# Four blocks of a two-turn macaron layer: transposes moved from TensorE to VectorE squares, with fewer steps in between

## The chip, the cores and the metric

The kernel runs on one core of a Trainium2 chip. The metric is the device time of one execution in microseconds (us). A core has engines that run side by side and meet at semaphores: TensorE (PE, matrix products; its weight loads are listed as PEld), VectorE (DVE), ScalarE (ACT), GpSimd (POOL) and SyncE (SP, which here only issues transfers). Transfers (DMAs) are issued by SP and by GpSimd. Matmul results land in PSUM, which holds eight banks of 128x512 fp32 numbers here; everything else lies in SBUF or in the chip's DRAM.

## What is computed

The input x has 4 sequences of 1024 positions with 256 features. The reference is three residual parts, each after a layer norm:

```
x = x + 0.5 * ffn(layernorm(x))
x = x + attn(layernorm(x))          # long convolution over positions, gelu, @ W.T + b
x = x + 0.5 * ffn(layernorm(x))     # the same weights as the first

def ffn(x):                         # weights are ternary, with one scale per output
    h = silu(lin(x, w1)) * lin(x, w2)     # 256 -> 1024
    h = gelu(lin(h, h1))                  # 1024 -> 1024
    h = gelu(lin(h, h2))                  # 1024 -> 1024
    return lin(h, w3)                     # 1024 -> 256
```

## The kernel before

**Two turns of eight blocks.** The 4096 positions are cut into 8 blocks of 512. The first turn ("f", names with _f) runs the first ffn over the eight blocks and leaves x1 in DRAM; the second turn ("g", names with _g) runs the last ffn on x2 and writes the output. The convolution part ("mixing", `mix`, one run per sequence of two blocks) turns x1 into x2; it is cut into small pieces that are put between the steps of the ffn of later blocks, by a planner (`tick`) that gives each step an allowance of 2500 units of work and counts every VectorE operation as 130 plus its columns. Checks that no weight is changed by the rounding to fp32r (`given`, `weight_checks`) fill what is left; their verdict passes through one small matmul, `p_bad`.

**The ffn of a block.** Activations are kept with features on the partitions and positions along the columns, as two fp32r parts: a rounded part, and the low part that is left over. `linear` (L355) makes an output tile of 128x512 from 2 x k matmuls, one per part and per 128 inputs. Layer 1 makes 8 pairs of tiles `pa`, `pb` from the block's normalized input `xt`; layers 2 and 3 make 8 tiles each, `p`, of 16 matmuls; the last makes `po`, 32 matmuls. After each tile of layers 2 and 3, ScalarE applies gelu (L388) and rounds (L390), and VectorE makes the low part (L293, `low_part`).

**Steps.** After each of these 16 tiles the ffn calls `ahead`, which moves the preparation of the next block on by one step: 16 steps, and a last one in front of `po`. `prepare` is a generator; each `yield` in it ends a step.

**Preparing a block.** It loads the next block's x, takes statistics, applies the root on ScalarE, scales (`norm`), and has to turn positions-by-features into features-by-positions, `xt`. There are two ways:

- *On TensorE* (`transposed`, L295). `load_rows` brings the block in one DMA, with 128 positions on the partitions. In the last step, eight 128x128 transposes into two PSUM banks `pt` (L302), then VectorE copies the rounded part out of PSUM (L312) and makes the low part (L293).
- *In squares* (`squares`, L317, and `parted`, L340). `load_x` brings the block in four DMAs of 128 KB, ordered so that VectorE's transpose of 32x32 squares puts each square where four stores to a DRAM buffer `moved` (L328, issued by GpSimd) can place it; after both halves, two loads `xf` (L336, GpSimd) bring features-by-positions back. In the last step VectorE rounds `xf` into `xt` (L345) and makes the low part (L293).

Before the change all blocks of the first turn but block 0, and the odd blocks of the second turn, are made in squares; the even blocks of the second turn (0, 2, 4, 6) are made on TensorE. Block 0 of the first turn is made on TensorE too, at the start of the kernel. The odd and the even blocks start at different steps, because mixing leaves x2 two blocks at a time: an odd block loads at once, an even one waits nine steps first. What one step issues:

| step | odd block, squares | even block, TensorE |
|---|---|---|
| 1 | load (4 DMAs) | |
| 4 | statistics, root | |
| 6 | scaling | |
| 8, 9 | square transposes, stores to `moved` | |
| 10 | | load (1 DMA) |
| 11 | loads of `xf` | |
| 13 | | statistics, root |
| 15 | | scaling |
| last | round, low part | 8 transposes, copies, low part |

The program is written in this order, but a scheduler puts each engine's instructions into a fixed order of its own, so that an instruction can stand earlier or later in its engine's queue than its step.

**Buffers.** `xb` (the loaded block) has 3 buffers, shared with the mixing's inputs; `half` tiles (among them `sq` and `xf`) 19, `ring` tiles (`xt` and the activations) 15, PSUM 8.

**Two programs in one.** If the weight checks find something, a second copy of the kernel with full fp32 arithmetic runs; with these inputs it doesn't.

Of the kernel before, what the change touches and what calls it, by code (L numbers as in the profile page):

```python
# [11 lines left out]
F32 = mybir.dt.float32  # L12
# [5 lines left out]
P = 128  # L18
B, L, D = 4, 1024, 256
HID = 1024  # L20
J = L // P
DC = D // P
KH = HID // P
TB = 512
JT = TB // P
# [72 lines left out]
def macaron_layers(  # L98
# [23 lines left out]
    nc = tc.nc  # L122
    split = bad is not None
# [3 lines left out]
    work = ctx.enter_context(tc.tile_pool(name="work", bufs=2))  # L127
# [21 lines left out]
    def bank(name):  # L149
        return psum.tile([P, 512], F32, tag="ps", name=name)  # L150

    def half(name, *shape, dtype=F32):

        return work.tile([P, *(shape or (512,))], dtype, tag="half", name=name, bufs=19)

    def ring(name, *shape, dtype=F32):

        return work.tile([P, *shape], dtype, tag="ring", name=name, bufs=15)
# [5 lines left out]
    ident = keep.tile([P, P], F32, name="ident")  # L164
# [14 lines left out]
    x2 = dram.tile([B, L, D], F32, name="x2")  # L179
# [17 lines left out]
    def block_of(t, blk):  # L197
        b, g = divmod(blk, J // JT)
        return t[b, g * TB : (g + 1) * TB, :]

    def tokens(t, blk, i=0, n=JT):

        return block_of(t, blk).rearrange("(i p) d -> p i d", p=P)[:, i : i + n, :]
# [3 lines left out]
        src = block_of(t, blk).rearrange("(n s) (q r) -> q s n r", s=SQ, r=SQ)  # L207
        return src[k * (P // SQ) + c]

    def load_rows(t, blk, name):  # L210

        xb = work.tile([P, JT, D], F32, tag="xb", name=name, bufs=3)
        nc.sync.dma_start(xb, tokens(t, blk))
        return xb

    def load_x(t, blk, name, queue=nc.sync):


        xb = work.tile([P, JT, D], F32, tag="xb", name=name, bufs=3)
        src = block_of(t, blk).rearrange("(i n s) d -> i s n d", i=JT, s=SQ)  # L220
        for i in range(JT):
            queue.dma_start(xb[i * SQ : (i + 1) * SQ], src[i])
        return xb
# [9 lines left out]
    x_first = work.tile([P, JT, D], F32, tag="xb", name="x_f0", bufs=3)  # L233
# [27 lines left out]
    def norm(t, name, parts_of=1):  # L261

        stats = small.tile([P, JT, 6], F32, tag="stats", name=f"stats_{name}", bufs=3)
        mv = small.tile([P, JT, 2], F32, tag="mv", name=f"mv_{name}", bufs=3)
        rstd = small.tile([P, JT], F32, tag="rstd", name=f"rstd_{name}", bufs=3)
        step = JT // parts_of
        for at in range(0, JT, step):
            here = range(at, at + step)
            for i in here:
                bn_stats(stats[:, i, :], t[:, i, :])  # L270
            for i in here:
                bn_aggr(mv[:, i, :], stats[:, i, :])
            nc.scalar.activation(
                rstd[:, at : at + step], mv[:, at : at + step, 1], AF.Sqrt, bias=eps
            )
        yield
        for at in range(0, JT, step):
            nc.vector.reciprocal(rstd[:, at : at + step], rstd[:, at : at + step])
            for i in range(at, at + step):
                ts(  # L280
                    t[:, i, :],
                    t[:, i, :],
                    mv[:, i, 0:1],
                    rstd[:, i : i + 1],
                    ALU.subtract,
                    ALU.mult,
                )
        yield


    def low_part(t, src):

        return nc.vector.tensor_tensor(t[:, 1, :], src, t[:, 0, :].bitcast(F32), ALU.subtract)  # L293

    def transposed(xn, name, first=False):  # L295

        pts = [bank(f"pt_{name}_{k}") for k in range(DC)]
        order = [(k, i) for k in range(DC) for i in range(JT)]  # L300
        for k, i in sorted(order, key=lambda o: o[1]) if first else order:
            nc.tensor.transpose(  # L302
                pts[k][:, i * P : (i + 1) * P], xn[:, i, k * P : (k + 1) * P], ident
            )
        xt = [ring(f"xt_{name}_{k}", parts, TB, dtype=wide) for k in range(DC)]
        last = None
        if first:
            last = nc.vector.tensor_copy(xt[0][:, 0, :], pts[0])  # L308
            nc.scalar.copy(xt[1][:, 0, :], pts[1])
        for k in range(DC):  # L310
            if not first:
                nc.vector.tensor_copy(xt[k][:, 0, :], pts[k])  # L312
            if split:
                last = low_part(xt[k], pts[k])
        return (xt, last) if first else xt

    def squares(xn, name):  # L317

        out = []
        for k in range(DC):
            sq = half(f"sq_{name}_{k}", P // SQ, JT, SQ)
            squares_of(
                sq, xn[:, :, k * P : (k + 1) * P].rearrange("p j (c r) -> p c j r", r=SQ)
            )
            for a in range(JT):
                stores.dma_start(  # L328
                    moved[k].rearrange("(c r) a q -> a r c q", r=SQ)[a],
                    sq[a * SQ : (a + 1) * SQ].rearrange("r c j s -> r c (j s)"),  # L330
                )
            yield
        yield
        for k in range(DC):
            t = half(f"xf_{name}_{k}")
            stores.dma_start(t, moved[k].rearrange("d a q -> d (a q)"))  # L336
            out.append(t)
        yield out

    def parted(xf, name):  # L340

        xt = []
        for k, src in enumerate(xf):
            t = ring(f"xt_{name}_{k}", parts, TB, dtype=wide)
            nc.vector.tensor_copy(t[:, 0, :], src)  # L345
            if split:
                low_part(t, src)
            xt.append(t)
        return xt
# [617 lines left out]
    def prepare(turn, blk, upcoming):  # L967

        name = f"{turn}{blk}"

        by_squares = turn == "f" or blk % 2 == 1
        if turn == "f":

            queue = weights_from if blk < 4 else nc.sync
            xb = x_second if blk == 1 else load_x(x, blk, f"x_{name}", queue)
        else:
            if not by_squares:
                for _ in range(9):
                    yield
            while ("m", blk // 2) not in done:  # L980
                next(aside, None)
            xb = (load_x if by_squares else load_rows)(x2, blk, f"x_{name}")
        yield
        yield
        yield
        for _ in norm(xb, name):
            yield
            yield
        if by_squares:
            for xf in squares(xb, name):  # L990
                yield
        while ("last layer", blk, turn) not in done:
            yield
        upcoming.extend(parted(xf, name) if by_squares else transposed(xb, name))

    def all_aside():

# [36 lines left out]
        nc.tensor.matmul(warm[:, 0:P], ident, ident, start=(i == 0), stop=(i == N_WARM - 1))  # L1034
    for _ in norm(x_first, "f0", parts_of=2):
        pass
    xt, last_split = transposed(x_first, "f0", first=True)
    allowed = work_done
    for n, (turn, blk) in enumerate(blocks):
        following = []  # L1040
        steps = [prepare(*b, following) for b in blocks[n + 1 : n + 2]]

        def ahead(last=False):
            for step in steps:
                if last:
                    done.append(("last layer", *blocks[n + 1][::-1]))
                next(step, None)

        src, dst = (x, x1) if turn == "f" else (x2, out)
        with tc.issue_after(last_split.ins) if n == 0 else nullcontext():  # L1050
            ffn(xt, src, dst, blk, f"{turn}{blk}", tick, ahead, n + 1 == len(blocks))
        done.append((turn, blk))
        xt = following
# [5 lines left out]
def macaron_kernel(tc: tile.TileContext, *args):  # L1059
    nc = tc.nc  # L1060
    with tc.tile_pool(name="flag", bufs=1) as flags:
        bad = flags.tile([1, 1], I32, name="bad")
        macaron_layers(tc, bad, *args)
        n_bad = nc.values_load(bad, min_val=0, max_val=1 << 24)
        with tc.If(n_bad > 0):
            macaron_layers(tc, None, *args)
# [65 lines left out]
```

## Time and profile before

| | |
|---|---|
| time, median of 3 runs | 1409.93 us (1409.23 to 1410.16) |
| the profiled execution | 1409.72 us |
| its span, first to last instruction | 1407.9 us |
| granted clock of TensorE | 0.999 of full speed |
| VectorE's 8 casts of `xt` from PSUM (L312) | 687 ns each |
| VectorE's 8 casts of `xt` from `xf`, second turn (L345) | 423 ns each |
| square transposes of 128x512, second turn | 705 ns each |
| GpSimd's issues to `moved`, second turn | 32, 551 ns each |
| matmuls of layers 2 and 3, second turn | 2048, 390 to 391 ns each |

The span is what the profile covers; the execution's own time is 1.82 us longer. A mean length isn't what an instruction holds an engine for: 390 ns is the length of a matmul from start to end, but they overlap, and 1024 of them are busy 236.5 us together, 0.23 us each. So for TensorE starts are compared with starts. "Idle before" and "waited" count the time in which an engine stood still ahead of an instruction, and name what released it.

In the second turn a block takes 79 to 94 us, which depends on how much mixing lies between its steps. VectorE is busy 48 to 63 us of each of the first four blocks, and about 26 us of block 6, which has no mixing.

### The profile page before, as it was taken

What the parts mean: (1) busy time and instruction counts of PE and PEld (TensorE: products, weight loads), DVE (VectorE), ACT (ScalarE), POOL (GpSimd) and SP (SyncE); (2) the same over time, 40 slices, a digit from 0 to 9 for tenths busy, and PEclk for the clock granted to TensorE, in tenths of its full rate; (3) what the DMA queues carried; (4) which work ended last, traced back from release to release, by engine and by line L of the source; (5) the groups of instructions that cost most, each with busy time, mean ns of one, the idle gap of its engine ahead of it and who ended that gap; (6) DMA issues with size and microseconds to landing.
All of it is one profiled execution on the core that took longest, in us unless ns stands there. A gap on an engine that the chain in (4) does not pass through costs nothing.

```text
span 1407.9 us, 17823 instructions
## 1 busy us (share of the span) xinstructions
PE 1397.6 (99%) x6524; PEld 1165.4 (83%) x6524; DVE 836.2 (59%) x1606; ACT 708.4 (50%) x1070; POOL 244.2 (17%) x358
## 2 busy tenths in 40 slices
PE   9999999999999999999999999999999999999997
PEld 7888888888888888888888888888888888888886
DVE  6896567755547784477673568744586744542412
ACT  5986479644546454344352553533545343553532
POOL 4221012211312120320113200214002122021200
PEclk9999999999999999999999999999999999999999
DMA  9401101122231322422113304034031223111000
GB/s 357 113 19 29 33 16 46 30 57 68 72 90 36 115 66 70 135 60 83 34 46 116 105 31 112 23 120 112 23 93 35 60 68 108 54 32 40 16 15 19
DMA packets 109282, 97.06 MB, mean 69 GB/s; under 512 B 71472, under 2 KB 81712, under 8 KB 109184
## 3 DMA queue, kind: packets, MB, share of 16 engines
q1 hardware_dynamic: 93056, 55.37, 14.3%
q0 software_dynamic: 15856, 40.19, 9.9%
q8 instruction: 53, 0.87, 0.3%
q14 instruction: 45, 0.37, 0.1%
q10 hardware_dynamic: 272, 0.26, 0.1%
HBM read 74.81 MB, written 20.97 MB: 68 GB/s over the span
## 4 chain that ended last, share of the span: by engine, by line
PE 99%; DVE 0%; POOL 0%; issue 0%; POOLq 0%
PE p_f L355 33%; PE p_g L355 33%; PE pa_f L355 4%; PE po_f L355 4%; PE pb_f L355 4%; PE pb_g L355 4%; PE pa_g L355 4%; PE po_g L355 4%; PE pi L916 2%; PE pw L941 2%; PE pf_m L738 2%; PE pk L665 1%; PE po_g L434 1%; PE pf_k L738 0%; PE warm L1034 0%; PE pt_g L302 0%
## 5 line engine op out<-in xcount | busy, mean ns | idle before, releaser
L355 PE MATMUL p_f<-h_f,h_sb 128*128 128x512 f32 x1024 | 237.2, 391 | 0.0
L355 PE MATMUL p_g<-ha_g,h_sb 128*128 128x512 f32 x1024 | 236.5, 391 | 0.0
L355 PE MATMUL p_g<-h_g,h_sb 128*128 128x512 f32 x1024 | 235.6, 390 | 0.0
L355 PE MATMUL p_f<-ha_f,h_sb 128*128 128x512 f32 x1024 | 235.3, 390 | 0.0
L293 DVE TENSOR_TENSOR h_g<-g_g,h_g 128x512 fp32r<-128x512 f32 x128 | 88.5, 692 | 246.5 <-ACT h_g L390 246.3
L388 ACT ACTIVATE g_g<-p_g,sc_sb 128x512 f32<-128x512 f32 x128 | 88.3, 690 | 275.9 <-PE p_g L355 268.9
L355 PEld LDWEIGHTS p_g<-ha_g,h_sb 128*128 128x128 f32 x1024 | 192.0, 188 | 40.5 <-DVE ha_g L293 0.9
L355 PEld LDWEIGHTS p_f<-h_f,h_sb 128*128 128x128 f32 x1024 | 191.8, 188 | 40.1 <-DVE h_f L293 0.3
L355 PEld LDWEIGHTS p_g<-h_g,h_sb 128*128 128x128 f32 x1024 | 192.0, 188 | 39.8
L355 PEld LDWEIGHTS p_f<-ha_f,h_sb 128*128 128x128 f32 x1024 | 191.9, 188 | 39.8
L388 ACT ACTIVATE g_f<-p_f,sc_sb 128x512 f32<-128x512 f32 x128 | 87.7, 689 | 188.9 <-PE p_f L355 188.5
L293 DVE TENSOR_TENSOR h_f<-g_f,h_f 128x512 fp32r<-128x512 f32 x128 | 87.8, 690 | 145.8 <-ACT h_f L390 145.4
L390 ACT CAST h_g<-g_g 128x512 fp32r<-128x512 f32 x128 | 79.4, 620 | 4.0
L390 ACT CAST h_f<-g_f 128x512 fp32r<-128x512 f32 x128 | 78.3, 618 | 3.0
L388 ACT ACT_TABLE_LOAD x51 | 65.4, 1283 | 25.0 <-PE p_f L355 14.3
L355 PE MATMUL pa_f<-xt_f,w_sb 128*128 128x512 f32 x256 | 69.1, 390 | 0.6 <-DVE xt_f L308 0.6
L417 POOL TENSOR_TENSOR y_g<-xr_g,y_g 128x512 f32<-128x512 f32 x14 | 18.1, 1294 | 293.1 <-DVE y_g L416 293.0
L355 PE MATMUL pb_f<-xt_f,w_sb 128*128 128x512 f32 x256 | 68.8, 389 | 0.0
L355 PE MATMUL pa_g<-xt_g,w_sb 128*128 128x512 f32 x256 | 68.4, 389 | 0.0
L355 PE MATMUL pb_g<-xt_g,w_sb 128*128 128x512 f32 x256 | 68.4, 389 | 0.0
L374 DVE SCALAR_TENSOR_TENSOR g_g<-pb_g,sc_sb,g_g 128x512 f32<-128x512 f32 x64 | 47.9, 749 | 27.8 <-PE pb_g L355 16.6
L328 POOL DMA_DIRECT2D moved<-sq_f x56 | 30.8, 556 | 182.9 <-DVE sq_f L140 182.9
(238 smaller groups left out, 1847.0 us busy)
## 6 DMA issues: line engine op xcount, KB each, us to landing
h_sb<-in_h_dram POOLq DMA_DIRECT2D x8, 1024.0 KB, 14.3
given<-in_h_dram SPq DMA_DIRECT2D x32, 256.0 KB, 3.8
kr<-k_hat SPq DMA_DIRECT2D x20, 256.0 KB, 2.6
ki<-k_hat SPq DMA_DIRECT2D x20, 256.0 KB, 2.9
xr_f<-in_x_dram SPq DMA_DIRECT2D x64, 64.0 KB, 2.4
x<-y_f POOLq DMA_DIRECT2D x64, 64.0 KB, 2.1
xm<-x SPq DMA_DIRECT2D x8, 512.0 KB, 3.7
m_m<-in_cosm_dram SPq DMA_DIRECT2D x16, 256.0 KB, 4.4
```

Source lines behind the costliest of these rows:

```text
L293: return nc.vector.tensor_tensor(t[:, 1, :], src, t[:, 0, :].bitcast(F32), ALU.subtract)
L328: stores.dma_start(moved[k].rearrange("(c r) a q -> a r c q", r=SQ)[a], sq[a * SQ : (a + 1) * SQ].rearrange("r c j s -> r c (j s)"),)
L355: nc.tensor.matmul(ps, w[:, k, m * P : (m + 1) * P], acts[k][:, part, :], start=(k == 0 and part == 0), stop=(k == n - 1 and part == parts ...
L374: nc.vector.scalar_tensor_tensor(g if split else t[:, 0, :], pb, sc_sb[:, 1, m : m + 1], g, ALU.mult, ALU.mult)
L388: nc.scalar.activation(g, ps, AF.Gelu, scale=sc_sb[:, layer, m : m + 1])
L390: nc.scalar.copy(t[:, 0, :], g)
L417: nc.gpsimd.tensor_tensor(y, rest[k], y, ALU.add)
L434: nc.tensor.matmul(ps[:, e * D : (e + 1) * D], ha[k][:, part, (i + e) * P : (i + e + 1) * P], w3_sb[:, k, :], start=(k == 0 and part == 0) ...
L665: nc.tensor.matmul(pk[0:NA, at + i, :, :].rearrange("p h b -> p (h b)"), a[:, i].rearrange("p a b -> p (a b)"), qd[d1 // per_tile][:, at + ...
L738: nc.tensor.matmul(ps[e][:, part, :], m[:, e, part, :], rows_of(q + JQ * e), start=True, stop=True)
L916: nc.tensor.matmul(banks[dc][e][:, q * P : (q + 1) * P], vs[q + JQ * e][:, part, dc * P : (dc + 1) * P], m[:, e, part, :], start=(part == ...
L941: nc.tensor.matmul(ps[:, e * D : (e + 1) * D], yts[dc][j // JQ][:, (j % JQ + e) * P : (j % JQ + e + 1) * P], wt_sb[:, dc, :], start=(dc == 0),
```

## The change

The even blocks of the second turn go the way of the odd ones: `load_x`, `norm`, `squares`, `parted`. To fit in, their preparation begins after seven steps and not nine, and some of the empty steps between its parts are left out: two steps and not three after the load, and one and not two after each half of `norm`. So an even block now loads at step 8, takes statistics at 10, scales at 11, transposes squares at 12 and 13, loads `xf` at 15, and rounds in the last step. The odd blocks' steps stay. `load_rows` goes, and `transposed` keeps only the form that block 0 of the first turn uses. The core of the diff:

```diff
-    def load_rows(t, blk, name):
-
-        xb = work.tile([P, JT, D], F32, tag="xb", name=name, bufs=3)
-        nc.sync.dma_start(xb, tokens(t, blk))
-        return xb
...
-        by_squares = turn == "f" or blk % 2 == 1
+        late = turn == "g" and blk % 2 == 0
         if turn == "f":
 
             queue = weights_from if blk < 4 else nc.sync
             xb = x_second if blk == 1 else load_x(x, blk, f"x_{name}", queue)
         else:
-            if not by_squares:
-                for _ in range(9):
+            if late:
+                for _ in range(7):
                     yield
             while ("m", blk // 2) not in done:
                 next(aside, None)
-            xb = (load_x if by_squares else load_rows)(x2, blk, f"x_{name}")
-        yield
-        yield
-        yield
+            xb = load_x(x2, blk, f"x_{name}")
+        yield
+        yield
+        if not late:
+            yield
         for _ in norm(xb, name):
             yield
+            if not late:
+                yield
+        for xf in squares(xb, name):
             yield
-        if by_squares:
-            for xf in squares(xb, name):
-                yield
         while ("last layer", blk, turn) not in done:
             yield
-        upcoming.extend(parted(xf, name) if by_squares else transposed(xb, name))
+        upcoming.extend(parted(xf, name))
```

The functions it calls, `load_x`, `norm`, `squares` and `parted`, are unchanged.

More of the change, by code (lines that the diff above doesn't have):

```diff
@@ L293, in low_part, with transposed @@
         return nc.vector.tensor_tensor(t[:, 1, :], src, t[:, 0, :].bitcast(F32), ALU.subtract)
-    def transposed(xn, name, first=False):
+    def transposed(xn, name):
         pts = [bank(f"pt_{name}_{k}") for k in range(DC)]
[L300 to L304, printed above, removed]
-        xt = [ring(f"xt_{name}_{k}", parts, TB, dtype=wide) for k in range(DC)]
[L306 to L313, printed above, removed]
+        for i in range(JT):
+            for k in range(DC):
+                nc.tensor.transpose(
+                    pts[k][:, i * P : (i + 1) * P], xn[:, i, k * P : (k + 1) * P], ident
+                )
+        xt = [ring(f"xt_{name}_{k}", parts, TB, dtype=wide) for k in range(DC)]
+        last = nc.vector.tensor_copy(xt[0][:, 0, :], pts[0])
+        nc.scalar.copy(xt[1][:, 0, :], pts[1])
+        if split:
+            for k in range(DC):
                 last = low_part(xt[k], pts[k])
-        return (xt, last) if first else xt
+        return xt, last
     def squares(xn, name):
@@ L1036, in macaron_layers @@
         pass
-    xt, last_split = transposed(x_first, "f0", first=True)
+    xt, last_split = transposed(x_first, "f0")
     allowed = work_done
```

## The prediction, made before the changed kernel ran

> **What bounds the kernel now.** I read the page first, then the waits of TensorE, then the timeline of the places where one block hands over to the next, on TensorE, VectorE and GpSimd.
>
> ```profile
> PE 1397.6 (99%) x6524; PEld 1165.4 (83%) x6524; DVE 836.2 (59%) x1606; ACT 708.4 (50%) x1070; POOL 244.2 (17%) x358
> ...
> PE 99%; DVE 0%; POOL 0%; issue 0%; POOLq 0%
> ```
>
> The first line is busy time by engine, the second the chain that ended last, by engine. TensorE is busy 1397.6 of 1407.9 us, and the chain is TensorE alone. The waits of TensorE say when it stood still for others:
>
> ```profile
> PE warm L1034 <- POOL ident masks.py:199: 2.6, 1, 2.6
> PE pa_f L355 <- DVE xt_f L308: 0.6, 1, 0.6
> ```
>
> That is all: 3.2 us, both at the start of the kernel. In the second turn TensorE never waits. So whatever leaves TensorE there comes off the time in full, as long as nothing that feeds it becomes late; and a wait elsewhere counts only from the point where TensorE runs dry.
>
> The change touches the handover. An even one (block 6 of the second turn is prepared), on TensorE, with start and length in us:
>
> ```profile
> 1228.44 3.94 PE L355 MATMUL p_g<-h_g,h_sb 128*128 128x512 f32 x16
> 1232.23 1.03 PE L302 MATMUL pt_g<-ident,x_g 128*128 128x128 f32 x8
> 1233.02 7.51 PE L355 MATMUL po_g<-h_g,w_sb 128*128 128x512 f32 x32
> 1240.37 1.07 PE L355 MATMUL pa_g<-xt_g,w_sb 128*128 128x512 f32 x4
> ```
>
> and an odd one (block 7), which is already made in squares:
>
> ```profile
> 1308.82 4.24 PE L355 MATMUL p_g<-h_g,h_sb 128*128 128x512 f32 x18
> 1312.90 7.42 PE L355 MATMUL po_g<-h_g,w_sb 128*128 128x512 f32 x32
> 1320.15 1.07 PE L355 MATMUL pa_g<-xt_g,w_sb 128*128 128x512 f32 x4
> ```
>
> Lengths overlap, so starts are to be compared. What follows layer 3 takes 1240.37 - 1232.23 = 8.14 us with transposes and 1320.15 - 1312.90 = 7.25 without. The odd one is a model of what every handover becomes.
>
> **What the Trainium skill says.** "TensorE: Matmul & The Clock Gate", Part 4: PE-mode transpose, gives about 275 ns for a transpose in a kernel's context, and says that its output goes to PSUM and needs a copy. The trace agrees on length (270 to 273 ns for pt_g), but eight of them hold the engine for only 0.79 us, some 0.1 each, as they are pipelined; the start-to-start figure is the price. "VectorE: DVE Perf Modes", The three transpose paths, says that VectorE transposes 32x32 blocks only; hence the squares need a trip through memory (`moved`). "DMA: Bandwidth & Descriptors", Anatomy of one DMA (SWDGE path), puts the fixed cost of a GpSimd transfer at about 2 us; the trace agrees (moved from sq_g 1.9 to 3.7, median 2.0; xf_g 2.8 to 3.7, median 3.0). The opening table of the first of these pages calls VectorE's queue strictly first in, first out. The trace agrees: in block 0 of the second turn a statistic waited 1.94 us for its load (782.09), and the next low part came only behind it (784.30). So a cast that waits for `xf` holds the low part behind it, and that is the wait that could reach TensorE.
>
> **The change part by part.** *Transposes on TensorE.* 4 blocks x 8 go. First transpose to first pa_g takes 8.16, 8.15, 8.17 and 8.14 us at the four even handovers (693.61 to 701.77, 875.45 to 883.60, 1057.28 to 1065.45, 1232.23 to 1240.37), mean 8.155, against 7.25 at the odd ones: 0.905 each, 3.62 us in all. Nothing hides them now, so all of it is gained.
>
> *VectorE.* Added per block: 2 square transposes, 0.705 each (sq_g row). The two casts read SBUF at 0.423 (L345) where they read PSUM at 0.687 (L312); low parts stay at 0.69. Net 1.41 - 0.53 = +0.88 per block, 3.5 us over four, on an engine with 41% idle: nothing. The 7.7 us of its waits for pt_g go too, which nobody waited for.
>
> *GpSimd.* 8 stores to `moved` at 0.551 and 2 loads of `xf` at 0.563 more per block, 5.5 us, 22 us over four on an engine that is 17% busy: nothing. In the built program no other GpSimd instruction stands between a block's first `moved` and its last `xf` at these four places. The y_g additions behind them wait for po_g, which comes later.
>
> *SP.* One load of 512 KB becomes four of 128 KB, about 0.43 us each to issue against 0.38: 1.3 us more on its queue; weights to be checked and residuals stand behind, with cover.
>
> *The timing with fewer steps.* A step is one output tile of layers 2 and 3, 16 matmuls, 3.63 us. In the new order the second square transpose comes behind the low part of layer 3's fourth tile (at most 1.7 us of other work between: three statistics and a weight check), the casts behind the seventh: three steps, 10.9 us. What must fit between is shown by block 7 now, on VectorE and GpSimd:
>
> ```profile
> 1286.07 0.70 DVE L140 STREAM_TRANSPOSE sq_g<-x_g 128x512 f32<-128x512 f32 x1
> ...
> 1310.85 0.69 DVE L293 TENSOR_TENSOR h_g<-g_g,h_g 128x512 fp32r<-128x512 f32 x1 [2.93 <-ACT h_g L390]
> 1311.46 0.76 DVE L345 CAST xt_g<-xf_g 128x512 fp32r<-128x512 f32 x2
> 1314.47 0.69 DVE L293 TENSOR_TENSOR h_g<-g_g,h_g 128x512 fp32r<-128x512 f32 x1 [2.26 <-ACT h_g L390]
> ```
>
> ```profile
> 1287.07 2.17 POOL L328 DMA_DIRECT2D moved<-sq_g  x4 [1.39 <-DVE sq_g L140]
> 1289.23 0.58 POOL L336 DMA_DIRECT2D xf_g<-moved  x1
> 1291.20 0.56 POOL L336 DMA_DIRECT2D xf_g<-moved  x1 [1.40 <-DMA moved<-sq_g]
> ```
>
> The first two figures of a line are start and length; the bracket is the idle time before and what ended it. From the end of the transpose (1286.77) to the second issue (1291.20) plus 3.0 to land: 7.4 us. Here there were 24.7 us before the cast. Afterwards, counted from the start of that fourth low part, the transpose ends at 1.3 to 3.0, `xf` lands at 8.7 to 10.4, and the cast's turn is at 10.9 + 0.6 = 11.5. It is in time by 1.1 to 2.8 us, thin but positive. If it is late by W, casts and the eighth low part follow: at the odd handover they would end at 1311.46 + W + 0.76 + 0.69 = 1312.9 + W, and po_g's last two of its first 16 need them at 1312.90 + 14 x 0.2266 = 1316.07. So W up to 3.1 us costs TensorE nothing, and the transfers may run 4.2 to 5.9 us longer than in block 7 before it stands still. I take 0; the bound above is below.
>
> *The mixing slides.* The square transposes count 2 x (130 + 512) = 1284 in the planner, half a step's allowance, so mixing work comes about one step later in odd blocks' neighbours: in the built order the pi matmuls of block 0 stand behind 8 steps, not 7; those of block 4 move into block 5; the flag's matmul p_bad moves into block 6. The groups are the same in number, and a 16-matmul group beside a mixing group takes 3.64 us against 3.63: nothing, and p_bad is still a block and a half from the end. Two covers get thinner. Block 2's statistics now stand ahead of block 1's casts; their data can be loaded when the last store of x2 has landed. Before block 6 that load was issued 6.7 us after the end of pw; with four issues (1.7) and landings of 2.7 to 5.8 it is there by 11 to 14 us, and its turn comes 4 steps and 2 us after pw, at 16.5. And two PSUM banks of pw now stay taken through block 3's first layer, leaving 6 of 8: three pairs of pa and pb at 1.81 us a pair, so a bank must come free within 3.6 us; at the start of block 7 the first pb, complete at about 1321.97, was read by 1323.83, in 1.9 us. Nothing for both.
>
> *Sum.* 1407.9 - 3.6 = 1404.3 of span. The profiled execution took 1409.72, 1.82 more than its span: 1406.1. It lies 0.2 under the median of 1409.93, so the median should be 1406.3.
>
> **The rivals.**
> - *`xf` comes late (the slower side).* The place is the cast in VectorE's queue at the four even handovers. The longest landings in the trace on GpSimd's queue are 5.6 us for `moved` and 5.6 for `xf`, both in the first turn, against 2.0 and 3.0: 6.2 us more, which passes the margin of 4.2 to 5.9 by 0.3 to 2.0 us. At the worst at all four: 8 us, 1414.3. It decides once the stalls pass 3.6 us in sum, 0.9 per handover. For it: the cover shrinks from 24.7 to about 9 us. Against: no xf_g landing took over 3.7, and TensorE never waited for one.
> - *A shifted wait takes back part.* Late statistics of block 2, or the two held banks: 1.5 us together at one handover, 1407.8. For it: in block 0 VectorE already waited 1.9 us for such a load. Against: the leads of 2.5 us and 1.7 us just worked out.
> - *The gap is filled by something else.* If po_g, now 0.8 us earlier, met the eighth low part late, half the gain would go: 1408.1. Against: the odd handovers run in 7.25 us with that very order.
>
> **How the numbers follow.** Forecast 0.76; shifted wait 0.11; gap filled 0.07; late `xf` 0.06. About 0.2% (2.8 us) is what a measurement of this kernel can tell from no change; the forecast clears it by only 0.8 us, so most of the second and third case is "same". Faster 0.77, same 0.18, slower 0.05. The range goes from 1405.5, for 0.8 us of noise and small gains, to 1408.3, which holds the second and third rival.
>
> **What would show it.** No pt_g in the profile but the first block's; at all eight handovers into blocks of the second turn 7.25 us from po_g to pa_g; TensorE's waits still two lines; busy TensorE about 1394. A wait of DVE xt_g for the DMA of xf_g under 3 us would be harmless, a wait of PE po_g or pa_g for DVE would prove me wrong at that place, and a po_g to pa_g stretch over 8.1 us would undo the gain there.

## The result, and the profile after

| | before | changed |
|---|---|---|
| median of 8 runs each | 1409.89 us (1409.23 to 1410.16) | 1405.70 us (1405.23 to 1406.43) |
| the profiled execution, and its span | 1409.72, 1407.9 | 1405.23, 1403.3 |
| the eight handovers of the second turn, in order | 8.16 7.25 8.15 7.25 8.17 7.25 8.14 7.25 | 7.55 7.26 7.25 7.25 7.25 7.25 7.26 7.26 |

The ratio of the times is 0.997, interval [0.996, 0.9979]: 4.2 us faster. The handovers are counted as in the prediction, from the end of layer 3 to the first `pa_g`.

The page of the changed kernel, whose lines answer to those of before:

```profile
PE 1393.0 (99%) x6492; PEld 1161.4 (83%) x6492; DVE 838.6 (60%) x1614; ACT 707.6 (50%) x1070; POOL 266.3 (19%) x398
...
PE 99%; DMA 1%; POOL 0%; DVE 0%; issue 0%; POOLq 0%
```

TensorE has 32 instructions less (6524 to 6492) and is busy 4.6 us less. VectorE and GpSimd carry 2.4 and 22.1 us more, and the chain that ended last is still TensorE. Its waits in the changed kernel (in total, times, longest):

```profile
PE warm L1024 <- POOL ident masks.py:199: 2.6, 1, 2.6
PE pa_f L344 <- DVE xt_f L299: 0.7, 1, 0.7
PE pa_f L344 <- DMA w_sb<-in_w_dram: 0.4, 1, 0.4
PE pt_f L295 <- DVE x_f L140: 0.2, 1, 0.2
```

All four are names of the first turn, and of block 0's start, which the change does not touch; the last two are not listed in a second profile of the same kernel (experiment 7). In the second turn no matmul is listed as waiting, before or after. The timeline of TensorE at the handover into block 6 (start, length) is now that of an odd block:

```profile
1228.89 7.42 PE L344 MATMUL po_g<-h_g,w_sb 128*128 128x512 f32 x32
1236.15 1.07 PE L344 MATMUL pa_g<-xt_g,w_sb 128*128 128x512 f32 x4
```

1236.15 - 1228.89 = 7.26, where before there were 8.14. At block 0 it is longer, by 0.3 us:

```profile
693.71 7.71 PE L344 MATMUL po_f<-h_f,w_sb 128*128 128x512 f32 x32
701.26 1.07 PE L344 MATMUL pa_g<-xt_g,w_sb 128*128 128x512 f32 x4
```

**Where the time went.** To leave out what lies at the two ends of the kernel, one stretch is used below: from the start of layer 2 in the last block of the first turn to the start of the last tile's `po_g` matmuls. Both are read from the chain of waits: 635.74 to 1392.85 before, 635.85 to 1388.99 after. So the stretch fell from 757.11 to 753.14, by 3.97 us. (The span fell by 4.5; 0.7 of that is what follows the stretch, and what lies ahead of it was 0.1 longer.) The handovers account for 4 x 0.905 - 0.30 = 3.32 of them. The other 0.64 are two stalls of TensorE that I had not seen. They stand in the waits of its weight loads, not in those of its matmuls. Before, from 636 us on:

```profile
PEld p_g L355 <- DVE ha_g L293: 0.9, 2, 0.4
```

and after, in the same window:

```profile
PEld po_f L344 <- DVE h_f L287: 0.4, 1, 0.4
...
PEld po_f L344 <- ACT h_f L379: 0.2, 1, 0.2
```

The line of before is gone, and the two of after are new: those are the 0.3 us at block 0. (Two lines that hold 0.4 and 0.2, `p_bad` and the last `po_g`, stand in both.) The figures of this view exceed what TensorE loses, so the loss is read from starts: at the entry to layer 2 of block 0, 112 matmuls in a row took 25.70 us before, and 25.39 in a kernel without the stall (experiment 3); at block 2, 176 took 40.22 against 39.89. The Trainium skill ("Perfetto Trace Analysis", Tensor Engine Instruction) says that TensorE can pull weight loads ahead of matmuls in flight; 0.9 us of waits for 0.64 lost, and 0.6 for 0.30, fit that, but no run tests it.

Sum: -3.62 - 0.64 + 0.30 = -3.96, against 3.97 measured. The rest of the 4.2 lies before and after the stretch, where executions of one and the same kernel differ by as much (last section).

What made the stalls is seen on VectorE. Before, as block 0 of the second turn enters layer 2:

```profile
718.47 0.18 DVE L278 RECIPROCAL rstd_m<-rstd_m 128x4 f32<-128x4 f32 x1 [0.57 <-ACT rstd_m L273]
718.69 0.74 DVE L140 TENSOR_SCALAR xm<-xm,mv_m,rstd_m 128x256 f32<-128x256 f32 x2
719.34 0.69 DVE L293 TENSOR_TENSOR ha_g<-g_g,ha_g 128x512 fp32r<-128x512 f32 x1
```

The last low part that layer 2 needs (719.34) stands behind the mixing's root and scaling, which fell just there. Their input's load (`xm`) was issued at 694.7, after the transposes at 693.61 had read the block's `xb` buffer for the last time; the mixing's input shares those three buffers. SyncE's own waits name the holder (from 670 to 730 us, kernel before):

```profile
SPq L193 <- PE pt_g L302: 4.3, 1, 4.3
```

Block 2 shows the same: the load at 876.5, behind a wait of 6.6 us for `pt_g`, and scaling at 900.51 ahead of the last low part (901.16). After the change the buffer was free when its squares were made, the load was issued at 682.7, and the statistics (689.24) and root came out of layer 1 into layer 3 of the block before. That removes the stalls. It also makes the new one, on ScalarE, between gelu and rounding of the eighth tile:

```profile
693.91 0.69 ACT L377 ACTIVATE g_f<-p_f,sc_sb 128x512 f32<-128x512 f32 x1 [2.28 <-PE p_f L344]
694.62 1.28 ACT L267 ACT_TABLE_LOAD   x1
695.91 0.30 ACT L267 ACTIVATE rstd_m<-mv_m,eps 128x4 f32<-128x4 f32 x1
696.12 0.60 ACT L379 CAST h_f<-g_f 128x512 fp32r<-128x512 f32 x1
```

The root needs another table, and rounding comes 1.5 us late. The eighth low part then ran from 696.75 to 697.44. In the program's order `po_f` takes the eighth tile's rounded part with its 15th matmul and the low part with its 16th, at 693.71 + 15 x 0.2266 = 697.11: 0.33 us too late. The length of the table load is what the Trainium skill gives ("ScalarE: Activation LUTs", What ACT_TABLE_LOAD costs: 1283 ns).

### The profile page after: what moved, and what is told of

Its sections match the earlier page's. It is cut to its first block, busy times and chain, and to the rows that moved or that the text cites. A ratio compares the mean times of both kernels' runs of the same rounds, so it can differ in the third digit from the quotient of the medians.

```text
span 1403.3 us, 17882 instructions
## 1 busy us (share of the span) xinstructions
PE 1393.0 (99%) x6492; PEld 1161.4 (83%) x6492; DVE 838.6 (60%) x1614; ACT 707.6 (50%) x1070; POOL 266.3 (19%) x398
## 4 chain that ended last, share of the span: by engine, by line
PE 99%; DMA 1%; POOL 0%; DVE 0%; issue 0%; POOLq 0%
PE p_f L344 33%; PE p_g L344 33%; PE po_f L344 4%; PE pa_g L344 4%; PE pb_g L344 4%; PE pa_f L344 4%; PE pb_f L344 4%; PE po_g L344 4%; PE pi L905 2%; PE pf_m L727 2%; PE pw L930 2%; PE pk L654 1%; PE po_g L423 1%; DMA w_sb<-in_w_dram 1%; PE pf_k L727 0%; POOL w_sb L238 0%
## 5 line engine op out<-in xcount | busy, mean ns | idle before, releaser
L317 POOL DMA_DIRECT2D moved<-sq_g x64 | 34.9, 552 | 330.3 <-DVE sq_g L140 290.7
L377 ACT ACT_TABLE_LOAD x51 | 65.4, 1283 | 26.0 <-PE p_f L344 14.3
```

The costliest lines, as they stand in the source:

```text
L317: stores.dma_start(moved[k].rearrange("(c r) a q -> a r c q", r=SQ)[a], sq[a * SQ : (a + 1) * SQ].rearrange("r c j s -> r c (j s)"),)
L377: nc.scalar.activation(g, ps, AF.Gelu, scale=sc_sb[:, layer, m : m + 1])
```

## The experiments

Each is set against the kernel before on the same chip; experiments 1 to 4 ran in one session, 5 to 8 in another. L numbers shift by a line or two with the edits, and are up to 11 lower in the changed kernel than in the one before. "The stretch" is that of the section above: 757.11 before, 753.14 changed.

**1. The transposes put back, without use.** Into the changed kernel, ahead of the rounding of `xf`:

```diff
         while ("last layer", blk, turn) not in done:
             yield
+        if late:
+            pts = [bank(f"pt_{name}_{k}") for k in range(DC)]
+            for k in range(DC):
+                for i in range(JT):
+                    nc.tensor.transpose(pts[k][:, i * P : (i + 1) * P], ident, ident)
         upcoming.extend(parted(xf, name))
```

> The changed kernel, with eight 128x128 transposes of the identity put back on TensorE at each of the four even handovers, into two PSUM banks that nobody reads; VectorE, GpSimd and SP do what they do in the changed kernel. It adds work that the output does not use. Theory A (the gain is the time that the transposes held TensorE): po_g to pa_g takes about 0.8 to 0.9 us longer at each even handover, 3.3 to 3.6 us in all, so 1409.0 to 1409.4, and a span 3.3 to 3.6 above the changed kernel's. Theory B (a good part of the gain came from the mixing that slid, the transposes themselves being cheap): under 2 us come back, at most 1407.7.

Measured: 1409.27 us (1408.35 to 1410.2), ratio 0.9994 [0.9986, 1.0002]. The even handovers are 8.15, 8.14, 8.17 and 8.14 again. TensorE at block 6:

```profile
1230.85 1.03 PE L988 MATMUL pt_g<-ident 128*128 128x128 f32 x8
...
1238.99 1.07 PE L344 MATMUL pa_g<-xt_g,w_sb 128*128 128x512 f32 x4
```

1238.99 - 1230.85 = 8.14, as before the change. The stretch is 756.45, 3.31 above the changed kernel: 3.62 for the transposes less the 0.30 at block 0, where the table load still stands between gelu and rounding but the transposes now cover it. And 756.45 is 0.66 below before, though TensorE does the same work as before: that part of the gain does not come from TensorE's transposes.

**2. The shift of the mixing alone.** The kernel before, in which an even block's second and third step after its load are charged the square transposes' units in the planner, so that the mixing slides as in the changed kernel:

```diff
+        if not by_squares:
+            work_done += OP_WORK + TB
         yield
+        if not by_squares:
+            work_done += OP_WORK + TB
         yield
```

> The kernel before, with transposes on TensorE as they were; only the planner counts 2 x 642 units more at the two steps at which the changed kernel makes its squares, so that the mixing slides as it does in the changed kernel. Theory A (the slide is worth nothing; the two short stalls of TensorE at the entry to layer 2 of blocks 0 and 2 went because the loaded block gives its buffer back earlier, which lets the mixing's input come earlier): no change, 1409.9 within 0.3, and both stalls (0.3 us each) are still there. Theory B (the slide took the stalls away, or more): 1409.3 or less, and the stalls are gone.

Measured: 1409.89 us (1409.46 to 1411.63), ratio 1.0 [0.9991, 1.0008]; the stretch is 757.13. Its weight loads between 700 and 910 us still wait for the same thing:

```profile
PEld p_g L355 <- DVE ha_g L293: 0.9, 2, 0.4
```

The mixing's matmuls stand after the same steps as in the changed kernel, so the edit does make the slide. Sliding the mixing by its planned work thus neither costs nor gains, and isn't what removed the stalls.

**3. The change without the shift.** The even blocks' square transposes are made without being counted by the planner:

```diff
-    def squares(xn, name):
+    def squares(xn, name, transpose=squares_of):
...
-            squares_of(
+            transpose(
...
-        for xf in squares(xb, name):
+        for xf in squares(xb, name, nc.vector.transpose if late else squares_of):
```

> The changed kernel, but the square transposes of the even blocks are not counted by the planner, so that the mixing stays where it was before the change. Theory A: the same gain as the changed kernel, 1405.4 to 1406.1, and the two stalls at the entry to layer 2 of blocks 0 and 2 stay gone, since the buffer is given back as early as in the changed kernel. Theory B: the stalls are back, and the gain is 0.6 us or more smaller, 1406.3 or more.

In the trace the mixing's matmuls stand where they stood before the change through block 3 of the second turn; the later ones (`pi`, `pw`, `p_bad`) still come one or two steps later than before, one earlier than in the changed kernel.

Measured: 1405.45 us (1404.76 to 1405.54), ratio 0.9966 [0.9952, 0.9979]. All eight handovers take 7.25 to 7.27, the two stalls are absent, and the stretch is 752.85, 0.29 below the changed kernel. ScalarE at the same place as above shows why (from its repetition, experiment 8):

```profile
694.51 0.62 ACT L379 CAST h_f<-g_f 128x512 fp32r<-128x512 f32 x1
...
697.81 0.30 ACT L267 ACTIVATE rstd_m<-mv_m,eps 128x4 f32<-128x4 f32 x1 [1.38 <-DVE mv_m L140]
```

The root now stands behind the rounding, and the eighth low part is in time.

**4. The squares at the last moment.** The changed kernel, started three steps later and without the empty steps around `xf`, to put a price on a late `xf`:

```diff
-                for _ in range(7):
+                for _ in range(10):
...
+        if not late:
+            yield
-        yield
...
-            yield
+            if not (late and xf):
+                yield
```

> The changed kernel with the even blocks' preparation three steps later and the empty step between squares and loads left out: squares at steps 15 and 16, xf loaded in the last step and cast at once. The second square transpose ends between 0.9 us before and 0.4 us after layer 3's last matmul; with 7.4 us to land, xf comes at 6.5 to 7.8 after it, and the first low part at 7.6 to 10, where pa_g asks for it at 7.5. Theory A (cover is worked off step by step; TensorE stands still only past it): stalls of 0.1 to 2.5 us at the four even handovers, 2 to 7 us in all, 1408 to 1413, shown as waits of pa_g for the DVE parts of xt_g, and none elsewhere. Rival (landing on GpSimd's queue is much longer when it collides with the stores of results): over 10 us in all. Rival (the path from squares to xt has slack that I don't see): under 1 us.

Measured: 1407.43 us (1406.67 to 1408.01), ratio 0.9981 [0.9972, 0.9989]; the stretch is 755.20, 2.06 above the changed kernel. So even here it stays faster than before; the loss lies at the low edge of what was expected, and the time 0.6 below it. Among the waits of TensorE's matmuls is a new one:

```profile
PE pa_g L345 <- DVE xt_g L335: 1.3, 2, 1.0
```

Against the kernel without the shift (752.86 in experiment 8) the stretch loses 2.34: 1.20 ahead of the first `pa_g` of block 0 (8.45 against 7.25), 0.81 within its layer 1 (15.31 from first `pa_g` to layer 2, against 14.50) and 0.33 at block 2. The last two of the four blocks lose nothing, where stalls were expected at all four. At block 0 GpSimd's second issue of `xf` was at 700.73 and the second cast at 703.81, where the changed kernel has them at 688.09 and 694.23 on. GpSimd had stood still for 4.06 us ahead of that issue, against 2.91, 2.04 and 1.40 at the other three blocks; the trace names a different releaser each time, so what held it longest at block 0 is open. What kept the loss small is argued from the order on VectorE: the scheduler had put the eighth low part (694.75) ahead of the casts (701.13), so `po_f` ran its 7.4 us while `xf` was on its way.

**5. A fourth buffer.** The kernel before, with one buffer more for `xb`, and one `ring` tile fewer to make room:

```diff
-        return work.tile([P, *shape], dtype, tag="ring", name=name, bufs=15)
+        return work.tile([P, *shape], dtype, tag="ring", name=name, bufs=14)
...
-        xb = work.tile([P, JT, D], F32, tag="xb", name=f"xm_{b}_{g}", bufs=3)
+        xb = work.tile([P, JT, D], F32, tag="xb", name=f"xm_{b}_{g}", bufs=4)
```

> The kernel before, transposes on TensorE and all, with a fourth buffer for loaded blocks (a ring tile is given up for the room). Theory (the two stalls of TensorE at the entry to layer 2 of blocks 0 and 2 come from the even block's buffer being held until the last step, which pushes the second statistics of the mixing's input into layer 1): both stalls go, 0.6 us from block 7 of the first turn to the last po_g, so 1409.3 within 0.4. Rival (the squares themselves or the planner took the stalls away): they stay, and the stretch stays at 757.1 us.

Measured: 1411.41 us (1410.93 to 1412.63), ratio 1.0012 [1.0005, 1.0018]. The expected time was missed: the stretch begins at 638.11 and not 635.74, since in the first turn layers 2 and 3 now wait once each:

```profile
PE p_f L355 <- DVE h_f L293: 1.1, 1, 1.1
...
PE p_f L355 <- DVE ha_f L293: 0.3, 1, 0.3
```

The second, in layer 2 of block 1, is the pattern of the stalls above: a table load, a root and the next block's scaling stand ahead of the last low part; from layer 2 to layer 3 that block takes 29.94 us against 29.01. The first, in layer 3 of block 6, costs 1.43 us. There one low part took 3.07 us and not 0.69, beside two additions on GpSimd:

```profile
580.37 2.53 POOL L957 TENSOR_TENSOR yw<-xr,yw 128x512 f32<-128x512 f32 x2
580.39 3.07 DVE L293 TENSOR_TENSOR h_f<-g_f,h_f 128x512 fp32r<-128x512 f32 x1 [1.36 <-ACT h_f L390]
```

In the kernel before, the same additions (576.79 to 579.33) end ahead of that low part (579.45). Whether the buffer more or the ring tile less moved these instructions isn't known: the run changed both.

The stretch itself, which the theory is about, takes 756.47: 0.64 below before. All its even handovers still cost 8.14 to 8.18. Its weight loads from 636 us on:

```profile
PEld p_bad L506 <- issue: 0.4, 1, 0.4
PEld po_g L434 <- DVE h_g L293: 0.2, 1, 0.2
```

The two waits for `ha_g` are gone, with the transposes and the steps as they were. The two loads of `xm`, issued at 609.1 and 694.7 before, now leave together, at 608.25. So it was the buffer, held to the last step, that kept the mixing's input back; the other edit, a ring tile less, only takes room away.

**6. Two steps later.** A milder form of experiment 4: the start moved by two steps, and the empty step ahead of the loads of `xf` left out for these blocks:

```diff
-                for _ in range(7):
+                for _ in range(9):
...
-        yield
+        if not late:
+            yield
```

> The changed kernel with the even blocks' preparation two steps later and the empty step between squares and loads left out, so squares at steps 14 and 15. In the built order the casts of xt_g now stand behind the eighth low part and not ahead of it. Theory (a late xf costs TensorE only past the end of po_g, since the order of VectorE is made with the landing in mind): xf lands 2.9 to 4.6 us after layer 3, the first low part is done by 6 to 7, in time for pa_g at 7.5: no wait of pa_g for xt_g, time as the changed kernel within 0.5 us, 1405.2 to 1406.2. Rival (the prediction's margin, 4.2 to 5.9 us beyond the lead of one block, is all that there is; 7.3 us later is past it): 1.4 to 3.1 us of stall per handover, 1411 or more.

Measured: 1406.62 us (1405.88 to 1407.41), ratio 0.9977 [0.9968, 0.9986]; the stretch is 753.48, 0.35 above the changed kernel. The time was 0.4 us over what was expected, and the rival's 1411 or more did not come. All handovers take 7.25 or 7.26. VectorE at block 0:

```profile
696.01 0.67 DVE L287 TENSOR_TENSOR h_f<-g_f,h_f 128x512 fp32r<-128x512 f32 x1
...
698.03 0.43 DVE L335 CAST xt_g<-xf_g 128x512 fp32r<-128x512 f32 x1 [0.74 <-DMA xf_g<-moved]
...
700.71 0.43 DVE L335 CAST xt_g<-xf_g 128x512 fp32r<-128x512 f32 x1 [0.99 <-DMA xf_g<-moved]
```

The casts do wait for `xf`, as the prediction's slow rival has it, but behind the low part and not ahead of it, so 0.7 and 1.0 us of waiting reach TensorE only in layer 1, which takes 15.16 us against 14.50. `pa_g` does wait there once for a low part of `xt_g` (0.4 us by the list of matmuls), where no such wait was expected.

**7 and 8. The changed kernel and the one without the shift again**, side by side.

> The changed kernel once more, beside the next one on the same chip. 1405.7 within 0.4, with 0.3 us of TensorE lost at the handover into block 0 of the second turn, where the root of the mixing's norm stands on ScalarE between gelu and rounding of the eighth tile.

> The changed kernel without the planner's count for the late squares, once more. Theory (it gains 0.3 us on the changed kernel by the order of ScalarE at one handover): 1405.4 within 0.4, 0.3 below the changed kernel, and the handover into block 0 takes 7.25 us from po_f to pa_g. Rival (its first figure was chance): the same as the changed kernel.

Measured: the changed kernel 1405.88 us (1405.05 to 1406.8), ratio 0.9973 [0.9963, 0.9983], stretch 753.13, block 0's handover 7.55 again; without the shift 1405.15 us (1404.89 to 1405.94), ratio 0.9968 [0.9956, 0.998], stretch 752.86, all handovers 7.25 to 7.27. The 0.3 us between them stood in the traces of both pairs. As times the two can't be told apart: the intervals overlap. By the stretch the version without the shift is the best that was run; by its time it is clear of the kernel before alone.

## Why the prediction was right, and where it was not

- *The transposes, 3.62 us.* Right, to a hundredth. Seven of the eight handovers are at 7.25 or 7.26, and putting the transposes back (experiment 1) puts 8.14 to 8.17 back.
- *"In the second turn TensorE never waits."* Wrong, and one of two terms that the sum put at nothing. It was read from the waits of TensorE's matmuls, which show none; its weight loads waited for `ha_g` twice. The change took 0.64 us with them, through the `xb` buffer, a part of the change that the prediction did not price at all. Experiment 5 removes them with a buffer more and the transposes kept, experiment 2 shows that the shift in the planner does not.
- *The mixing slides: "nothing".* Right for the shift by itself (experiment 2: 757.13 against 757.11). In the changed kernel, where the mixing's input comes earlier too, it put the root with its table load ahead of a rounding, and cost 0.30 us at block 0; take the shift out and that is gone (experiments 3 and 8). The two covers that were worked out, block 2's statistics and the PSUM banks, show no wait in the trace.
- *The rival "the gap is filled by something else".* It came true in small and at one of four handovers: the eighth low part met `po` late, and 0.30 us and not half the gain went. The prediction argued against it from the odd handovers' order on VectorE; the cause sat on ScalarE. It also has the low part wanted at 14 matmuls into `po`; that is the rounded part's place, and the low part's is one matmul, 0.23 us, later.
- *The cover of `xf`.* Predicted 1.1 to 2.8 us. In the changed kernel the lead of the second landing over the cast, with 3.0 us to land, is 3.1, 3.2, 2.1 and 1.2 us at the four blocks, and nobody waited for `xf`. At the thinnest, block 6, GpSimd issued it at 1223.28 and the cast began at 1227.50: 4.22 less 3.0. The landings of `xf` took 2.8 to 3.7.
- *"If it is late by W, casts and the eighth low part follow."* Not so where it was tried: with a later program order the scheduler put the low part first (experiments 4 and 6). There a late `xf` cost 0.6 and 2.3 us over the stretch (753.48 and 755.20 against 752.86), and the slow rival's 8 us were further off than its price said. The margin of 4.2 to 5.9 us, which holds for the order as built, was not tested: no transfer was ever slow enough.
- *VectorE and GpSimd.* +3.5 us predicted on VectorE, +2.4 measured (why it is less wasn't looked for); +22 on GpSimd, +22.1 measured. TensorE lost nothing to either sum.
- *The sum.* -3.6 predicted; the stretch gave -3.97 and the medians -4.2. That it came so near is in part luck: the two terms put at nothing, -0.64 and +0.30, half cancel.

## What to carry to other kernels

Where TensorE is the bound, read the waits of its weight loads beside those of its matmuls, and check a loss by comparing the starts of equal runs of matmuls: a stall can show in the one list and not in the other, and neither list has its size (in experiment 4 the matmuls' list holds 1.3 us where 2.34 were lost). When a step is rewritten, list what it holds (buffers above all) and for how long, not only what it issues: whatever shares the pool can move with it; here that gained 0.64 us at two places and cost 0.30 at another. And an instruction's place in a queue that a scheduler makes is not a constant: a margin worked out for one built order need not be that of the next.

## What the runs showed of the hardware

**Low parts on VectorE beside additions on GpSimd.** The ten traces have 4160 low parts on VectorE (`TENSOR_TENSOR` of 128x512). Those beside which GpSimd ran no addition took at most 0.70 us. 36 took over 0.80, up to the 3.07 of experiment 5, and every one of them lay beside such an addition; in 31 of the 36 the length is the time that they ran side by side plus 0.56 us, as if VectorE had stood still meanwhile. No run was made to test this. In the changed kernel there are four, up to 1.71 us long, and none of TensorE's waits is put down to them.

**The two ends of an execution.** Between executions of one kernel the long stretch repeats to a hundredth (753.14 and 753.13; 752.85 and 752.86), but the two ends do not. From the end of the last VectorE instruction to the end of the span it was 6.2 us before (1401.28 + 0.42 to 1407.9), 5.5 in the changed kernel's profiled execution and 6.2 in the same kernel's second one; and the stretch began anywhere from 635.17 to 635.85 in kernels whose first turn is the same. That is as large as the effects told apart here. What makes it wasn't looked for.
